# A channel-attention and depthwise-convolution kernel: transposes and head products laid between convolution products, attention's channels turned by 96

## The chip, the cores and the metric

The kernel runs on one core of one Trainium2 chip. Times are device microseconds (us) of one execution. The time before is 2817.3 us, the median of three runs (2817.22 to 2821.58). One further execution was taken with the hardware profiler; all lines with the name of an engine in them come from that one.

## What is computed

The input x has 384 channels of 192 x 192 pixels in float32. The program has two layers, each added to its own input:

```
n   = groupnorm(x, 32 groups)
qkv = 1x1 convolution of n, 384 -> 1152 channels
qkv = max over 2x2 pixels              # 96 x 96 pixels remain
qkv = depthwise 3x3 convolution
q, k, v = split(qkv)                   # 384 channels each, 8 heads of 48
attn = (q/|q|) @ (k/|k|)^T * temperature       # 48 x 48 for each head
out  = sum over 4 of  softmax(top-k of attn) @ v * a
x   = x + 1x1 convolution of repeat2x2(gelu(out)), 384 -> 384
x   = x + depthwise 7x7 convolution(groupnorm(x))
```

The attention matrix is between channels, not pixels: for each head a 48 x 48 matrix that is summed over all 9216 pooled pixels. Only after the last pixel can attention be applied to v.

## The kernel before, in words

Channels lie on the 128 partitions, so 384 channels are three tiles, `KT = 3`. The work comes in stages.

The first stage (to about 170 us) reads x for the statistics of the first norm and scales the 1x1 weights `wq` by them.

The **q/k stage** (to 1355 us) goes over 24 blocks of 8 image rows (`NB = 24`), in the loop `for b in range(NB + 1)`, and in each over six channel tiles `ct` (three of q, three of k). `pooled` makes the 1x1 convolution: three groups of 512 pixels, each three matrix products of 128 x 128 by 512 (L639) that add up in one PSUM tile `pq` (four buffers), and then a maximum over 2 x 2 pixels on VectorE (L647) into a ring of rows. A product in float32 appears in the trace as two instructions, a transpose as one. `depthwise` runs one block behind: nine multiply-adds on VectorE (L680, L682) give the tile `qk` of 128 channels by 384 pixels (nine buffers). When all six tiles of a block are there, `products` (L687 to L717) follows: ScalarE squares each of them for the norms (L691); then for each of three groups of 128 pixels TensorE transposes q's three tiles and k's three tiles into PSUM (L700, tile `tr`, three buffers), ScalarE copies each three to SBUF (L706, tiles `qkT0` and `qkT1`, two buffers each), and TensorE multiplies them (L709) into `grams`. The constant `SPAN` says which k channels a tile of 128 q channels meets: heads are 48 wide and don't end at 128, so the three products of a pixel group have 144, 192 and 144 columns. They add up in one PSUM bank over all blocks.

The loop's last turn (`b == NB`) has no q/k block to convolve. Its depthwise tiles and products remain, and six products of the v stage (`convolve`, tile `xv_begun`) are begun there.

`attention` (L769 to L862) turns `grams` into weights: a row of scales for k along the free dimension (`rkb`), scaled grams, ten small DMAs that bring each head's 48 columns to its q rows (`att`), ranks by comparing all pairs, four masked softmaxes mixed into `mix`, ten DMAs that lay them block-diagonally into `diag`, and seven transposes whose results are copied to `attnT`. It is a generator whose steps are written between the v products of the first three row blocks.

The **v stage** (to about 2195 us) goes over 16 row blocks, six groups of two image rows each, in an order that begins at row block 13 (`FIRST`). For each there are nine `convolve` calls (L537, three for each pair of groups) with a maximum on VectorE (L543), the depthwise 3x3 (L905, L909), `attend` (L961): for each half of the pixels and each tile of output channels the products of `attnT` with those tiles of v that hold a head in common, then gelu on ScalarE (L968); `project` (L985), the residual sum (L1022) and writes to HBM. The list `near` says which tiles meet: channel tiles 0, 1 and 2 meet two, three and two tiles of v, seven products for each half, each of 288 columns. Here most of the order is written by hand: `keep` is `tc.keep_in_program_order`, and the loop over `i` lists what follows what on TensorE and VectorE. The last three row blocks of attention lie behind the loop.

The **last stage** makes the second norm and the 7x7 convolution as matrix products (L1428).

Where `keep` isn't used, the tile framework orders the instructions of each engine when it builds the program, from its own estimate of what is ready; each engine then runs its list in order. `tc.issue_after(ins)` puts an engine's instructions behind `ins`.

The core of the products before is this:

```
for mt, (lo, hi) in enumerate(SPAN):
    last = nc.tensor.matmul(
        gram[mt],
        sides[0][:, mt * P : (mt + 1) * P],
        sides[1][:, lo:hi],
        start=False, ...
```

Of the kernel before, what the change touches and what calls it, by code (L numbers as in the profile page):

```python
# [8 lines left out]
F32 = mybir.dt.float32  # L9
AF = mybir.ActivationFunctionType  # L10
ALU = mybir.AluOpType
AX = mybir.AxisListType

P = 128
C = 384
KT = C // P
# [5 lines left out]
HC = C // HEADS  # L22
# [4 lines left out]
NB = PS // PR  # L27
IR = 2 * PR
BLK = IR * HW
PB = PR * PS  # L30
SUB = BLK // 512
NX = 3
GN_EPS = 1e-5


SPAN = []
for _mt in range(KT):
    _lo = (_mt * P) // HC * HC
    _hi = ((_mt + 1) * P - 1) // HC * HC + HC
    SPAN.append((_lo, _hi))  # L40

PIECES = []
for _mt in range(KT):
# [29 lines left out]
UT = 2  # L73
# [5 lines left out]
def conv_preact_d2(  # L79
# [17 lines left out]
    nc = tc.nc  # L97
# [16 lines left out]
    ident = const.tile([P, P], F32, name="ident")  # L114
# [31 lines left out]
    wp = const.tile([P, KT, C], F32, name="wp")  # L146
# [79 lines left out]

    ssq = const.tile([P, 2 * KT, NB], F32, name="ssq")
    attnT = const.tile([P, KT, C], F32, name="attnT")


    bctx = ExitStack()
# [26 lines left out]

    psx = ExitStack()
    pgram = psx.enter_context(tc.tile_pool(name="pgram", bufs=1, space=PSUM))  # L260
    gram = []
    for mt, (lo, hi) in enumerate(SPAN):
        o = sum(h - l for l, h in SPAN[:mt])
        gram.append((o, o + hi - lo))
    grams = pgram.tile([P, gram[-1][1]], F32, name="grams")
    gram = [grams[:, lo:hi] for lo, hi in gram]
    ptr = psx.enter_context(tc.tile_pool(name="ptr", bufs=3, space=PSUM))
    qx = ExitStack()
    pq = qx.enter_context(tc.tile_pool(name="pq", bufs=4, space=PSUM))
# [19 lines left out]
    keep = tc.keep_in_program_order  # L289
    with tc.tile_pool(name="stp", bufs=1) as stp, tc.tile_pool(name="xsp", bufs=5) as xsp:  # L290
# [19 lines left out]
        whole = stp.tile([P, P], F32, name="whole")  # L310
# [175 lines left out]
        w = wq[:, TWO, i * C : (i + 1) * C]  # L486
        nc.scalar.mul(w, w, rstd0[:, TWO : TWO + 1])
    with tc.issue_after(loaded):
        nc.sync.dma_start(wp, wprojT.rearrange("(t p) o -> p t o", p=P))

# [58 lines left out]
    with ExitStack() as bx:  # L551
        padp = bx.enter_context(tc.tile_pool(name="padp", bufs=1))
        qkp = bx.enter_context(tc.tile_pool(name="qkp", bufs=9))
        trp = bx.enter_context(tc.tile_pool(name="trp", bufs=2))

        gwp = bx.enter_context(tc.tile_pool(name="gwp", bufs=1))

# [66 lines left out]
        for ct in range(2 * KT):  # L624
            ring.append(padp.tile([P, 3 * PR + 2, PS + 2], F32, name=f"ring{ct}"))

        def pooled(b, ct, xb):
            rows = xb.rearrange("p t (r c) -> p t r c", c=HW)
            t = ring[ct]
            r0 = 1 + b % 3 * PR  # L630
            for g in range(3):
                begun, there = sums_qk.pop((b, ct, g), (None, False))
                ps = begun
                if not there:
                    ps = pq.tile([P, 512], F32, name=f"pq{b}_{ct}_{g}", tag="pq")
                    if begun is not None:
                        nc.scalar.copy(ps, begun)
                for kt in range(KT) if begun is None else (TWO,):
                    nc.tensor.matmul(  # L639
                        ps,  # L640
                        wq[:, kt, ct * P : (ct + 1) * P],
                        rows[:, kt, :, g * 64 : (g + 1) * 64],
                        start=(kt == 0),
                        stop=(kt == KT - 1),
                        skip_group_check=begun is not None,
                    )
                nc.vector.tensor_reduce(  # L647
                    t[:, r0 : r0 + PR, 1 + g * 32 : 1 + (g + 1) * 32],
                    ps.rearrange("p (h a w b) -> p h w a b", h=PR, a=2, b=2),
                    AX.XY,  # L650
                    ALU.max,
                )
# [32 lines left out]
            r0 = b % 3 * PR  # L685
            taps(dst, ct, lambda i, j: ring[ct][:, r0 + i : r0 + i + PR, j : j + PS])

        def products(b, qk):
            for i in range(2 * KT):
                junk = trp.tile([P, PB], F32, name=f"junk{b}_{i}", tag="junk")  # L690
                nc.scalar.activation(  # L691
                    junk, qk[i].rearrange("p h w -> p (h w)"), AF.Square,
                    accum_out=ssq[:, i, b : b + 1],
                )
            for j in range(PB // P):
                sides = []
                for s in range(2):
                    ps = ptr.tile([P, C], F32, name=f"tr{b}_{j}_{s}", tag="tr")
                    for i in range(KT):
                        nc.tensor.transpose(  # L700
                            ps[:, i * P : (i + 1) * P],
                            qk[s * KT + i].rearrange("p h w -> p (h w)")[:, j * P : (j + 1) * P],
                            ident,
                        )
                    sb = trp.tile([P, C], F32, name=f"qkT{b}_{j}_{s}", tag=f"qkT{s}")
                    nc.scalar.copy(sb, ps)  # L706
                    sides.append(sb)
                for mt, (lo, hi) in enumerate(SPAN):
                    last = nc.tensor.matmul(  # L709
                        gram[mt],  # L710
                        sides[0][:, mt * P : (mt + 1) * P],
                        sides[1][:, lo:hi],
                        start=False,
                        stop=(b == NB - 1 and j == PB // P - 1),
                        skip_group_check=True,
                    ).ins
            return last  # L717


        nc.tensor.matmul(  # L720
            grams, z[:, RUN : RUN + P], z[:, RUN : RUN + grams.shape[1]], start=True, stop=False,
            skip_group_check=True,
        )
        for b in range(NB + 1):
            xb = None
            if b < NB:
                xb = held.pop(b) if b in held else load_x(b, "xq")
            else:

                qx.close()  # L730
                pv = psx.enter_context(tc.tile_pool(name="pv", bufs=2, space=PSUM))
                xb = xpool.tile([P, 2 * UT, KT, RB * HW], F32, name="xv_begun", tag="xb")
                for kt in range(KT):
                    nc.sync.dma_start(xb[:, :, kt], image_rows(kt, order[0], 0, 2 * UT))
            qk = []
            for ct in range(2 * KT + 1):
                if b < NB and ct < 2 * KT:
                    if b == 0 and ct < 2:

                        if ct == 0:  # L740
                            pooled(b, 0, xb)
                            pooled(b, 1, xb)
                            biases()
                    else:
                        pooled(b, ct, xb)
                    bordered(b, ct)
                if b > 0 and ct > 0:
                    dst = qkp.tile([P, PR, PS], F32, name=f"qk{b}_{ct}", tag="qk")
                    qk.append(dst)
                    depthwise(b - 1, ct - 1, dst)  # L750
                    if ct == 2 * KT:
                        multiplied = products(b - 1, qk)
                    if b == NB:
                        with tc.issue_after(multiplied):
                            for n in ((), (), (0, 1), (), (2, 3), (4,), (5,))[ct]:
                                t0 = n // KT * UT
                                convolve(0, t0, n % KT, xb[:, t0 : t0 + UT], lambda ins: ins)
            if b == 2:
                for tiles in vrows:
                    row_borders(tiles)  # L760
            if b < len(pieces):
                with tc.issue_after(stats0):
                    weights(*pieces[b])

    xctx.close()

    near = {}

    def attention(ap):  # L769

# [13 lines left out]
        along_free(rkb, rn[:, KT : 2 * KT], ptr, "rk", "tr")  # L784
        yield

        scaled = ap.tile([P, KT, C // 2], F32, name="scaled")
        for mt, (lo, hi) in enumerate(SPAN):
            nc.vector.scalar_tensor_tensor(
                scaled[:, mt, 0 : hi - lo], gram[mt], rn[:, mt : mt + 1], rkb[:, lo:hi],  # L790
                ALU.mult, ALU.mult,
            )
        att = ap.tile([P, KT, HC], F32, name="att")
        for i, (mt, r0, r1, h) in enumerate(PIECES):
            eng = (nc.gpsimd, nc.scalar)[i % 2]
            o = h * HC - SPAN[mt][0]
            eng.dma_start(att[r0:r1, mt, :], scaled[r0:r1, mt, o : o + HC])
        yield


# [50 lines left out]
            eng.dma_start(diag[r0:r1, mt, h * HC : (h + 1) * HC], mix[r0:r1, mt, :])  # L851
        yield
        for dt in range(KT):
            cts = [ct for ct in range(KT) if SPAN[ct][0] < (dt + 1) * P and SPAN[ct][1] > dt * P]
            near[dt] = cts
            ps = ptr.tile([P, C], F32, name=f"aT{dt}", tag="tr")
            for ct in cts:
                nc.tensor.transpose(
                    ps[:, ct * P : (ct + 1) * P], diag[:, ct, dt * P : (dt + 1) * P], ident
                )  # L860
            lo, hi = cts[0] * P, (cts[-1] + 1) * P
            nc.vector.tensor_copy(attnT[:, dt, lo:hi], ps[:, lo:hi])  # L862

# [85 lines left out]
    def attend(i, pin=lambda ins: ins):  # L951
# [2 lines left out]
        gl = gp.tile([P, KT, PBC], F32, name=f"gl{b}", tag="gl")  # L954
        for h in range(2):
            for ct in range(KT):
                dts = [dt for dt in range(KT) if ct in near[dt]]
                ps = ptr.tile([P, C], F32, name=f"po{b}_{ct}_{h}", tag="tr")
                for dt in dts:
                    keep(  # L960
# [563 lines left out]
```

## Time and profile before

| what | before |
|---|---|
| median of three runs | 2817.3 us |
| the profiled execution | 2802.07 us |
| its span, first to last instruction | 2800.4 us |
| TensorE clock granted, mean | 0.994 |
| q/k transposes (L700) | 432 instructions, 273 ns each in the middle |
| gram products (L709) | 432 instructions: 288 of 144 columns, 144 of 192 |
| copies of transposes (L706) | 144 on ScalarE, 478 ns each |
| attention times v (L961) | 448 instructions of 288 columns |
| projection (L985) | 576 instructions of 288 columns |

A row of groups gives line, engine, operation, the tile written and those read, shapes and count, then busy time and the mean duration of one in ns, then idle time of the engine ahead of it and what ended it. On TensorE the instructions are pipelined: the duration of one is longer than the distance from its start to the next one's start, and that distance is what it costs in a full stream. A row of the timeline gives start, length, engine, line and count; neighbours of one kind are merged. PEld is TensorE's loading of the stationary operand, which can run beside a product.

### The profile page before, as it was taken

Reading aid. Unit: us, or ns where it says so; the run is one execution under the profiler, and the core shown is the slowest. Engines: PE = TensorE matmul, PEld = TensorE weight load, DVE = VectorE, ACT = ScalarE, POOL = GpSimd, SP = SyncE. Lnnn points to the kernel's source line nnn. Section 1 sums busy time; section 2 is a strip of 40 time slices with the busy share of each in tenths; the row PEclk is TensorE's granted clock in tenths of the full one; section 3 lists DMA queues with packets and bytes.
Section 4 is the critical chain, followed back from the end, with each engine's and each line's share of the span. In section 5 each row is a group of like instructions: output and inputs, shape, how many; then the busy total and the mean of one; then the engine's idle time right before and its main releaser. Section 6 shows DMA issues by size and latency. Waiting matters only on the chain. (4 is left out here: it accounts for less than half of the span.)

```text
span 2800.4 us, 25638 instructions
## 1 busy us (share of the span) xinstructions
PE 2646.0 (94%) x8717; PEld 1588.6 (57%) x8717; DVE 2324.8 (83%) x3383; ACT 873.3 (31%) x1638; POOL 748.0 (27%) x884
## 2 busy tenths in 40 slices
PE   0399999999999999999999999999999899999998
PEld 0144444445445444444556666666666677777776
DVE  7989887887878878878798988889889678887786
ACT  0141111111111111111202232222323577777776
POOL 1023443100000000000102231010101477877777
PEclk9999999999999999999999999999999999999999
DMA  9976666401001001010235998575664899999998
GB/s 381 400 248 216 227 203 219 165 34 68 34 34 68 34 35 67 34 62 7 78 127 174 334 379 314 171 249 196 209 236 152 321 341 360 374 367 370 367 376 265
DMA packets 234002, 580.98 MB, mean 207 GB/s; under 512 B 16608, under 2 KB 165712, under 8 KB 217104
## 3 DMA queue, kind: packets, MB, share of 16 engines
q1 hardware_dynamic: 173376, 283.44, 28.8%
q0 software_dynamic: 37376, 148.85, 15.2%
q10 hardware_dynamic: 23120, 147.07, 14.0%
q8 instruction: 69, 1.13, 0.2%
q14 instruction: 61, 0.50, 0.0%
HBM read 370.93 MB, written 208.21 MB: 207 GB/s over the span
## 5 line engine op out<-in xcount | busy, mean ns | idle before, releaser
L639 PE MATMUL pq<-xq,wq 128*128 128x512 f32 x2268 | 990.7, 593 | 0.0
L639 PEld LDWEIGHTS pq<-xq,wq 128*128 128x128 f32 x2268 | 423.9, 190 | 491.3 <-issue 446.5
L682 DVE SCALAR_TENSOR_TENSOR qk<-ring,wd,qk 128x384 f32<-128x384 f32 x1152 | 674.8, 613 | 20.9 <-ACT ring L669 7.1
L537 PE MATMUL pv<-xv,wq 128*128 128x384 f32 x1656 | 539.8, 487 | 2.5 <-DVE rows L543 1.4
L647 DVE TENSOR_REDUCE ring<-pq 128x128 f32<-128x512 f32 x428 | 293.9, 688 | 193.5 <-PE pq L639 192.0
L1428 PE MATMUL pc<-main,w 128*128 128x288 f32 x1536 | 436.2, 407 | 3.9 <-POOL aux L1348 1.7
L537 PEld LDWEIGHTS pv<-xv,wq 128*128 128x128 f32 x1656 | 314.8, 190 | 218.6 <-DVE rows L543 3.0
L1448 DVE TENSOR_SCALAR apart<-pc,rb 32x576 f32<-32x576 f32 x384 | 312.2, 813 | 108.9 <-PE pc L1428 97.1
L1428 PEld LDWEIGHTS pc<-main,w 128*128 128x128 f32 x1536 | 290.8, 190 | 87.3 <-issue 2.1
L1446 ACT ACTIVATE apart<-pc,rb 32x576 f32<-32x576 f32 x384 | 281.1, 732 | 137.2 <-PE pc L1428 132.4
L905 DVE SCALAR_TENSOR_TENSOR vb<-rows,wd,vb 128x576 f32<-128x576 f32 x384 | 313.2, 817 | 11.2
L1428 PE MATMUL pc<-aux,h 128*128 128x288 f32 x768 | 249.5, 407 | 3.1 <-issue 2.4
L691 ACT ACTIVATE junk<-qk 128x384 f32<-128x384 f32 x144 | 75.3, 523 | 544.0 <-DVE qk L682 544.0
L1387 POOL COPY res<-apart 128x1152 f32<-128x1152 f32 (+1 forms) x96 | 218.4, 2305 | 48.6 <-DMA out_dram<-res 40.2
L773 POOL TENSOR_TENSOR rn<-rn,halfpos 128x6 f32<-128x6 f32 x1 | 1.4, 1360 | 850.6 <-DVE rn L772 850.6
L1022 DVE TENSOR_TENSOR sx<-xr,y 128x576 f32<-128x576 f32 x180 | 203.7, 1173 | 26.9 <-ACT y L993 21.2
L1063 POOL DMA_DIRECT2D sd<-sx x96 | 72.2, 755 | 491.8 <-DVE sx L1022 472.6
L543 DVE TENSOR_REDUCE rows<-pv 128x192 f32<-128x768 f32 x144 | 137.8, 957 | 55.7 <-PE pv L537 55.6
L1428 PEld LDWEIGHTS pc<-aux,h 128*128 128x128 f32 x768 | 145.6, 190 | 45.2 <-issue 4.4
L1042 ACT ACTIVATE wq<-sx,negmid 128x1152 f32<-128x1152 f32 x96 | 120.6, 1256 | 95.4 <-DVE sx L1022 91.2
L1271 DVE SCALAR_TENSOR_TENSOR w<-eye,sb,w 128x512 f32<-128x512 f32 x96 | 144.1, 1540 | 1.5
L985 PE MATMUL pr<-gl,wp 128*128 128x288 f32 x576 | 142.6, 407 | 0.0
(226 smaller groups left out, 2113.6 us busy)
## 6 DMA issues: line engine op xcount, KB each, us to landing
sd<-sx POOLq DMA_DIRECT2D x96, 600.0 KB, 9.9
out_dram<-res SPq DMA_DIRECT2D x192, 288.0 KB, 10.7
main<-sd ACTq DMA_DIRECT2D x46, 1200.0 KB, 5.1
xv<-in_x_dram SPq DMA_DIRECT2D x138, 384.0 KB, 6.5
xr<-in_x_dram SPq DMA_DIRECT2D x45, 1152.0 KB, 12.0
xq<-in_x_dram SPq DMA_DIRECT2D x21, 2304.0 KB, 8.2
w<-wt ACTq DMA_DIRECT2D x46, 1024.0 KB, 6.9
xs<-in_x_dram SPq DMA_DIRECT2D x24, 1536.0 KB, 15.6
```

What stands on the lines that cost most here:

```text
L537: nc.tensor.matmul(ps[:, u, 0 : RB * HW], wq[:, kt, o : o + P], xb[:, u, kt, :], start=(kt == 0), stop=(kt == KT - 1),)
L639: nc.tensor.matmul(ps, wq[:, kt, ct * P : (ct + 1) * P], rows[:, kt, :, g * 64 : (g + 1) * 64], start=(kt == 0), stop=(kt == KT - 1), skip ...
L647: nc.vector.tensor_reduce(t[:, r0 : r0 + PR, 1 + g * 32 : 1 + (g + 1) * 32], ps.rearrange("p (h a w b) -> p h w a b", h=PR, a=2, b=2), AX. ...
L682: nc.vector.scalar_tensor_tensor(dst, src, w, dst, ALU.mult, ALU.add)
L905: pin(nc.vector.scalar_tensor_tensor(dst, src, w, dst, ALU.mult, ALU.add))
L985: nc.tensor.matmul(ps[:, 0:H], wp[:, ct, ot * P : (ot + 1) * P], gl[:, ct, h * H : (h + 1) * H], start=(ct == 0), stop=(ct == KT - 1),)
L1022: nc.vector.tensor_tensor(bass.AP(flat.tensor, flat.offset + at(e) + a * RUN, [flat.ap[0], [JP, NT], [1, NJ], [at(f) - at(e), 2]],), xq[:, ...
L1271: nc.vector.scalar_tensor_tensor(mid, eye.unsqueeze(1).to_broadcast([P, 4, P]), sb[:, c : c + 1], mid, ALU.mult, ALU.add,)
L1387: keep(copy(res[ps, k], apart[ps, :, k].rearrange("p e n -> p n e")))
L1428: nc.tensor.matmul(ahead[q][:, k, 0 : NT * NJ], lhs, rhs, start=(j == 0), stop=(j == 2), skip_group_check=True,)
L1446: keep(nc.scalar.mul(dst, src, scale))
L1448: keep(nc.vector.tensor_scalar_mul(dst, src, scale))
```

## The change

For q and k, products are now taken of two heads at a time: `PAIR` is 96 channels, and 96 q channels meet exactly the same 96 k channels, so a pixel group has four products of 96 x 96 for the three before. The result lies in partitions 0 to 95 of `grams`, four pairs side by side in 384 columns.

`products` is split. `squares` follows each depthwise tile. `turned` (the transposes and copies) and `products` become generators, put into a list `between`; `pinned` keeps the q/k convolution products in program order and takes one step of the list behind each of them: one transpose, or one product. The three q tiles of a block are transposed behind the first channel tile of the block after next's convolution, the k tiles behind the fourth, the twelve products behind those. The transposed sides hold a whole block (three pixel groups) in one buffer each. In the last turn the block before the last one's steps lie between the begun v products, and the last block's come after them in one go.

For v, the output channels of attention are turned by 96 (`TURN`): tile 0 holds channels 96 to 223, tile 1 224 to 351, tile 2 352 to 383 and 0 to 95. Each then meets two tiles of v (`MEET`), six products for each half. `attnT` is cleared once and written only where heads lie, and the rows of the projection's weights are loaded in the turned order by three DMAs. In `attention` the scaling by k's norms is one operation on 96 partitions, and the scaling by q's norms comes after the ten DMAs.

```diff
+PAIR = 2 * HC
+TURN = PAIR
+MEET = [...]
...
+    nc.gpsimd.memset(attnT, 0.0)
...
-    gram = [grams[:, lo:hi] for lo, hi in gram]
+    grams = pgram.tile([P, C], F32, name="grams")
...
-        nc.sync.dma_start(wp, wprojT.rearrange("(t p) o -> p t o", p=P))
+        whole = (C - TURN) // P
+        nc.sync.dma_start(
+            wp[:, 0:whole], wprojT[TURN : TURN + whole * P].rearrange("(t p) o -> p t o", p=P)
+        )
+        over = C - TURN - whole * P
+        nc.sync.dma_start(wp[0:over, whole], wprojT[C - over :])
+        nc.sync.dma_start(wp[over:P, whole], wprojT[0:TURN])
...
-        trp = bx.enter_context(tc.tile_pool(name="trp", bufs=2))
+        trp = bx.enter_context(tc.tile_pool(name="trp", bufs=1))
...
+        between = []
+        def pinned(ins):
+            if ins.ins.engine != mybir.EngineType.PE:
+                return ins
+            keep(ins)
+            while between and next(between[0], between) is between:
+                between.pop(0)
+            return ins
...
+                    if b > 1:
+                        pinned(ins)
...
+        def squares(b, ct, t):
+            junk = trp.tile([P, PB], F32, name=f"junk{b}_{ct}", tag="junk")
+            nc.scalar.activation(junk, t, AF.Square, accum_out=ssq[:, ct, b : b + 1])
+        def turned(b, s, side, qk):
+            for j in range(PB // P):
+                ps = ptr.tile([P, C], F32, name=f"tr{b}_{j}_{s}", tag="tr")
+                for i in range(KT):
+                    keep(
                         nc.tensor.transpose(
+                            ps[:, i * P : (i + 1) * P], qk[i][:, j * P : (j + 1) * P], ident
                         )
+                    )
+                    if i == KT - 1:
+                        nc.scalar.copy(side[:, j], ps)
+                    yield
+        def products(b, sides):
+            nonlocal multiplied
+            for j in range(PB // P):
+                for lo in range(0, C, PAIR):
+                    multiplied = keep(
+                        nc.tensor.matmul(
+                            grams[0:PAIR, lo : lo + PAIR],
+                            sides[0][:, j, lo : lo + PAIR],
+                            sides[1][:, j, lo : lo + PAIR],
+                            start=False,
...
+                    ).ins
+                    yield
...
+            done, qk = qk, []
             for ct in range(2 * KT + 1):
+                for s, at in enumerate((0, KT) if b < NB else (0, KT + 1)):
+                    if ct == at and done:
+                        if s == 0:
+                            sides = []
+                        sides.append(
+                            trp.tile([P, PB // P, C], F32, name=f"qkT{b}_{s}", tag=f"qkT{s}")
+                        )
+                        between.append(turned(b - 2, s, sides[s], done[s * KT : (s + 1) * KT]))
+                        if s == 1:
+                            between.append(products(b - 2, sides))
...
-                        with tc.issue_after(multiplied):
-                            for n in ((), (), (0, 1), (), (2, 3), (4,), (5,))[ct]:
-                                t0 = n // KT * UT
-                                convolve(0, t0, n % KT, xb[:, t0 : t0 + UT], lambda ins: ins)
+                        for n in ((), (), (0, 1), (), (2, 3), (4,), (5,))[ct]:
+                            t0 = n // KT * UT
+                            convolve(0, t0, n % KT, xb[:, t0 : t0 + UT], pinned)
+                        if ct == 2 * KT:
...
+                            for s in range(2):
+                                between.append(turned(b - 1, s, sides[s], qk[s * KT :]))
+                            between.append(products(b - 1, sides))
+                            for left in between:
+                                for _ in left:
+                                    pass
...
-            nc.vector.scalar_tensor_tensor(
-                scaled[:, mt, 0 : hi - lo], gram[mt], rn[:, mt : mt + 1], rkb[:, lo:hi],
-                ALU.mult, ALU.mult,
-            )
+        nc.vector.tensor_tensor(scaled[0:PAIR], grams[0:PAIR], rkb[0:PAIR], ALU.mult)
...
-            eng.dma_start(att[r0:r1, mt, :], scaled[r0:r1, mt, o : o + HC])
+            o = mt * P - h // 2 * PAIR
+            eng.dma_start(att[r0:r1, mt, :], scaled[o + r0 : o + r1, h * HC : (h + 1) * HC])
+        nc.vector.tensor_tensor(
+            att, att, rn[:, 0:KT].unsqueeze(2).to_broadcast([P, KT, HC]), ALU.mult
+        )
...
-            nc.vector.tensor_copy(attnT[:, dt, lo:hi], ps[:, lo:hi])
+            for l, h in ((lo, min(hi, TURN)), (max(lo, TURN), hi)):
+                if l < h:
+                    o = (l - TURN) % C
+                    nc.vector.tensor_copy(attnT[:, dt, o : o + h - l], ps[:, l:h])
...
-                dts = [dt for dt in range(KT) if ct in near[dt]]
+                dts = MEET[ct]
```

## Prediction

> **What bounds the kernel now.** First the page's engine shares and slices. From the third slice on TensorE (PE) is full at full clock, in the q/k stage (to 1355 us) and in the v stage (to 2133 us); VectorE (DVE) is below it.
>
> ```profile
> PE 2646.0 (94%) x8717; PEld 1588.6 (57%) x8717; DVE 2324.8 (83%) x3383; ACT 873.3 (31%) x1638; POOL 748.0 (27%) x884
> PE   0399999999999999999999999999999899999998
> PEclk9999999999999999999999999999999999999999
> ```
>
> Then the waits of q/k (window 200 to 1355): DVE waits for PE, PE for nearly nothing.
>
> ```profile
> DVE ring L647 <- PE pq L639: 187.8, 129, 1.9
> DVE qk L682 <- ACT ring L669: 7.1, 21, 0.3
> ```
>
> So time is PE's count of columns, and I read prices as differences of neighbouring starts. The timeline of PE around two block ends (start, length, count):
>
> ```profile
> 741.92 1.50 PE L700 MATMUL tr<-ident,qk 128*128 128x128 f32 x10
> 743.25 1.02 PE L639 MATMUL pq<-xq,wq 128*128 128x512 f32 x2
> 744.12 0.49 PE L700 MATMUL tr<-ident,qk 128*128 128x128 f32 x3
> ...
> 792.96 1.50 PE L700 MATMUL tr<-ident,qk 128*128 128x128 f32 x10
> ...
> 795.48 1.02 PE L639 MATMUL pq<-xq,wq 128*128 128x512 f32 x2
> 796.53 0.44 PE L700 MATMUL tr<-ident,qk 128*128 128x128 f32 x2
> ...
> 797.67 1.84 PE L709 MATMUL grams<-qkT,qkT 128*128 128x144 f32 x12
> 799.34 0.49 PE L700 MATMUL tr<-ident,qk 128*128 128x128 f32 x3
> 799.67 0.60 PE L639 MATMUL pq<-xq,wq 128*128 128x512 f32 x1
> ```
>
> Two convolution instructions take 0.86 us (743.25 to 744.12), so 0.429 each; a product in f32 is two instructions. Three transposes take 0.33 us, so 0.109 each, one instruction. The twelve gram instructions take 1.67 us: eight of 144 columns at 0.122 and four of 192 at 0.162 (their rows' means, 291 and 327 ns, differ by the same 0.04) are 1.62, the rest is a wait. A block lasts 51.04 us (741.92 to 792.96); first and last block end lie at 230.19 and 1355.53, so the mean is 1125.34 / 22 = 51.15.
>
> In v the same view gives 0.243 us for an instruction of 288 columns and 0.323 for 384; one row block lasts 50.35 us, all PE:
>
> ```profile
> 1589.27 6.96 PE L961 MATMUL po<-vb,attnT 128*128 128x288 f32 x28
> 1596.06 11.78 PE L537 MATMUL pv<-xv,wq 128*128 128x384 f32 x36
> 1607.67 8.89 PE L985 MATMUL pr<-gl,wp 128*128 128x288 f32 x36
> 1616.40 23.38 PE L537 MATMUL pv<-xv,wq 128*128 128x384 f32 x72
> 1639.62 0.65 PE L961 MATMUL po<-vb,attnT 128*128 128x288 f32 x2
> ```
>
> The windows of v (engine sums, then clock, DMA share, GB/s) show the one other full resource, in two row blocks:
>
> ```profile
> 1588.00:1639.00 51.00, 51.00 (x176) 33.13 (x175) 45.60 (x53) 13.76 (x30) 18.62 (x25) 1.00 1.04 383
> 1742.00:1792.00 50.00, 50.00 (x173) 32.53 (x172) 44.79 (x51) 13.77 (x30) 4.50 (x6) 1.00 0.63 211
> ```
>
> **What the Trainium skill says.** "TensorE: Matmul & The Clock Gate", section LDWEIGHTS: loading takes the weight's columns over 1.2 GHz whatever its rows, so 0.107 us for 128 and 0.080 for 96. The trace agrees for 128: thirty one-column bias products (176.71 to 179.98 us) take 0.109 each, so the load sets the pace. No load of 96 columns is in this trace. Same page, Part 2, step 1: the next load is pulled ahead under the running matmul. The trace agrees: after a transpose a convolution starts 0.109 us later, its load hidden. Same page, Part 1, "Architectural detail", engine queue depths: ScalarE (ACT) is strict FIFO; this matters for a rival. "Perfetto Trace Analysis", Roofline: 16 DMA engines give a core some 435 GB/s at most; the 383 above with a share of 1.04 is near it.
>
> **q and k, the work itself.** A block now is 108 convolution instructions x 0.429 = 46.33, 18 transposes x 0.109 = 1.96, and 3 x 2 x (0.122 + 0.162 + 0.122) = 2.44 of grams: 50.73. The mean is 51.15, so 0.42 are waits at the block's end for copies and last taps (as from 795.48 to 796.53 above: 1.05 us for two convolution instructions, 0.86).
> Added: 12 products of 96 columns for 9. The rows fit 0.833 ns per column plus 0.002 to 0.003, so one instruction streams in 0.083. Laid singly between convolutions, the first of the pair is followed by its own second half's load of 96 columns (0.083), the second by a convolution's load of 128, which 0.083 doesn't hide: 0.112. So 0.195 a product, 12 x 0.195 = 2.34: only 0.10 less than now. Bounds: if a 96-column load costs as much as 128, 0.224 each, 2.69; if loads hide wholly, 0.166, 1.99.
> Transposes are as many; 0.109 holds beside convolutions already. Waits: operands are a block old and the copies spread over the block, but the first product stands one convolution (0.86 us) behind the last k transpose, whose copy takes 0.48 on ACT plus pipeline. I keep half of today's, 0.21; bounds 0.05 and 0.60. New block: 46.33 + 1.96 + 2.34 + 0.21 = 50.84, 0.31 less. 22 blocks have their products laid in: **7 us** (bounds: 22 x (51.15 - 51.58) = -9 and 22 x (51.15 - 50.33) = +18).
> Squares are now written behind their own channel tile: same count on ACT, which already takes them as DVE finishes each tile. DVE's 41 of 51 us are unchanged. The q/k tiles' nine buffers suffice, since the q tiles are read in the first of six channel tiles.
>
> **The turn from q/k to v.** From the last q/k convolution's end (1355.5) to the end of the six v products begun there (1393.0) are 37.5 us. After: 72 x 0.323 = 23.3; 36 transposes 3.9; 12 products laid in 2.3; 12 in a row at 2 x 0.083, 2.0; the small temperature and norm products that lie there now 1.5; 1.0 for the last maxima, as v takes over their PSUM before any transposes cover it; 0.9 for copies at the drain, whose six at 0.43 outlast the transposes. Sum 34.9: **2.6 us** (0 to 5). If cover fails there, DVE's last q/k taps (1375) are late next; they end before the drain. The attention chain now starts with those products done, some 4 us later against PE's v products; today its matrix is ready at 1478.5 and first used at 1488.6, so that slack covers it.
>
> **v.** Six products for seven per half: 2 x 2 x 0.243 = 0.97 us per row block, 13 row blocks in the loop: 12.6. DVE has 44.8 of then 49.4 us and is next late, not yet. Two row blocks run at a DMA share of 1.04 (a 2 us wait for an input tile at 1668 follows); there a shorter PE only waits, so I take off 1.9: **10.7** (bounds 8 and 12.6). The last three row blocks (2133 to 2193) wait for DVE and ACT: 0.3 of 2.9.
>
> **Small things at nothing.** Clearing attnT on POOL is 1.07 us (the row of the equal diag memset) before the first statistics, while PE waits 97 us for input; without that cover 1.1. Projection weights in three DMAs for one: SP's queue at 166 us, the next q/k load is gated by blocks ending at 230; uncovered about 1 us. Attention's scaling: one operation for three (0.97), plus a multiply of 128x144 (0.3, as L829 of that shape), five small copies for three, within the chain's slack.
>
> **Sum.** 7 + 2.6 + 10.7 + 0.3 = 20.6. The profiled execution took 2802.07 us (span 2800.4, 1.7 around it), so 2781.5; the three runs' median lies 15.2 above it, which I take as unchanged: 2817.3 - 20.6 = **2796.7**.
>
> **Rivals.**
> - A, all covers hold, loads hide, waits vanish: 18 + 5 + 12.6 + 2.9 = 38, 2779. For it: PE's spacings are regular to a few nanoseconds. Against: the 0.109 floor of the bias products.
> - B, q/k gives nothing: loads at 0.112 and waits of 0.42 make 22 x (51.15 - 51.40) = -6; with 2 and 10: 2811. For: no 96-column load was seen.
> - C, slower: the ACT queue. A copy of the last k transposes falls behind a square, which waits for its taps; PE, now in a fixed order, stands at the first product and all convolutions queue behind it. For: ACT idles 544 us ahead of squares waiting for DVE, and a copy (L706) did run right behind a square (L691) that it had no need of:
>
> ```profile
> 744.87 0.52 ACT L691 ACTIVATE junk<-qk 128x384 f32<-128x384 f32 x1 [1.37 <-DVE qk L682]
> ...
> 745.61 0.86 ACT L706 COPY qkT<-tr 128x384 f32<-128x384 f32 x2
> ```
>
> Against: waits at block ends, this among them, cost PE 0.42 us in all. From 20.6 / 22, 0.94 us per block beyond my 0.21, it eats the whole gain; half a tile's taps (2.7 us) gives 59 - 21 = 38 slower, 2855.
> - D, v gives nothing, as DVE's order or DMA sets the row block: 2817.3 - 9.9 = 2807. Against: DVE's waits in v are for PE.
>
> **How the numbers follow.** Forecast 0.62, A 0.10, B 0.12, C 0.08, D 0.08. Two parts in a thousand (5.6 us) is about what can be told from no change. B's and D's tails fall within that; a third of B and an eighth of D are put there, the rest of them at faster: faster 0.62 + 0.10 + 0.08 + 0.07 = 0.87, same 0.05, slower 0.08. The range 2782 to 2811 takes in the forecast with the inner part of its bounds, D and half of B, and leaves out A's end and C.
>
> **What would show it.** Block period 50.6 to 51.0; gram instructions starting 0.083 and 0.112 apart; waits of PE for copies under 0.3 per block; row blocks of 49.4, the two at full DMA still 50.3 or with waits; turn near 35. Gram spacings of 0.112 both mean B; a recurring wait of PE for qkT over 1 us means C.

## The result and the profile after

The changed kernel took 2806.5 us (median of seven runs, 2803.1 to 2807.6) beside 2817.3 for the kernel before: a ratio of 0.9954, 95% interval 0.9938 to 0.9971, so 11 us were gained by the medians (8 to 17 by the interval) where 20.6 were forecast. Later both ran once more, on another chip: the kernel before took 2798.4 and the changed one 2785.7, 0.9953 again (0.9940 to 0.9965), a gain of 12.7 us. The experiments below ran on that chip and on a third; neither kernel ran again on the first. Ratios below are against the kernel before in the same session.

TensorE is still full; the gap in its 24th slice is new. From the page of the changed kernel:

```profile
PE 2630.5 (94%) x8797; PEld 1555.7 (55%) x8797; DVE 2328.5 (83%) x3383; ACT 874.2 (31%) x1638; POOL 752.8 (27%) x885
PE   0399999999999999999999979999999899999998
```

In q/k (waits of VectorE, window 200 to 1348) VectorE waits for TensorE as before, and for the transposes' reading of its old tiles, L725, which is new and costs TensorE nothing:

```profile
DVE ring L673 <- PE pq L663: 185.6, 106, 2.2
DVE qk L706 <- PE tr L725: 18.0, 43, 0.8
DVE qk L708 <- ACT ring L695: 4.7, 14, 0.3
```

TensorE's timeline in a block (start, length, count) shows what lies between:

```profile
772.69 0.27 PE L725 MATMUL tr<-ident,qk 128*128 128x128 f32 x1
772.80 1.02 PE L663 MATMUL pq<-xq,wq 128*128 128x512 f32 x2
773.66 0.33 PE L739 MATMUL grams<-qkT,qkT 128*96 128x96 f32 x2
773.83 1.05 PE L663 MATMUL pq<-xq,wq 128*128 128x512 f32 x2
774.72 0.33 PE L739 MATMUL grams<-qkT,qkT 128*96 128x96 f32 x2
```

A transpose costs 0.11 (772.69 to 772.80). A pair product takes 0.17 to the next convolution, but that one then takes 0.89 (773.83 to 774.72) and not 0.86: start by start, 0.083 and 0.085 for the product's two instructions, and 0.458 for 0.429 between the convolution's two. The sum, 0.083 + 0.085 + 0.029, is 0.197. The period is 50.72 in every block (51.15 before), and TensorE's waits for copies in q/k are gone.

In v the row block is as forecast, until 1650. Starts of TensorE, 1583.70 to 1633.08 being 49.38:

```profile
1583.70 5.98 PE L1014 MATMUL po<-vb,attnT 128*128 128x288 f32 x24
1589.52 11.77 PE L549 MATMUL pv<-xv,wq 128*128 128x384 f32 x36
1601.13 8.89 PE L1038 MATMUL pr<-gl,wp 128*128 128x288 f32 x36
1609.86 23.38 PE L549 MATMUL pv<-xv,wq 128*128 128x384 f32 x72
1633.08 5.98 PE L1014 MATMUL po<-vb,attnT 128*128 128x288 f32 x24
...
1650.51 8.89 PE L1038 MATMUL pr<-gl,wp 128*128 128x288 f32 x36
1676.47 1.62 PE L549 MATMUL pv<-xv,wq 128*128 128x384 f32 x2 [17.06 <-DMA xv<-in_x_dram]
1681.08 1.65 PE L549 MATMUL pv<-xv,wq 128*128 128x384 f32 x2 [3.00 <-DMA xv<-in_x_dram]
1685.55 24.71 PE L549 MATMUL pv<-xv,wq 128*128 128x384 f32 x68 [2.82 <-DMA xv<-in_x_dram]
```

Three waits for an input tile, 22.9 us, where the profile of before had 1.1 (27.6 and 1.9 when the late starts around them are counted). The late starts are products at a lower granted clock (the rate that TensorE was given): the two at 1676.47 take 1.62 us, and such a pair took 0.81 at 1350.85. The clock is the column ahead of the DMA share in this line:

```profile
1660.00:1692.00 32.00, 9.71 (x16) 4.60 (x17) 5.53 (x6) 3.96 (x10) 5.88 (x8) 0.57 1.04 370
```

The window 1560 to 1700 of the first profile of before, then of after:

```profile
1560.00:1700.00 140.00, 138.85 (x475) 89.88 (x474) 123.02 (x138) 40.70 (x88) 46.83 (x63) 1.00 1.00 362
```

```profile
1560.00:1700.00 140.00, 117.12 (x380) 73.38 (x379) 102.33 (x115) 35.24 (x74) 43.47 (x59) 0.90 0.99 341
```

DMA is full in both, but moved 6% less in the second. It moved less ahead of the first wait already: from 1584 to 1633 it was 364 GB/s, where the same kernel in the same window later moved 388 on the other chip (shares 1.03 and 1.04).

### The profile page after: what moved, and what is told of

The parts are those of the page before. It is cut to its first block, busy times and chain, and to the rows that moved or that the text cites. A ratio compares the mean times of both kernels' runs of the same rounds, so it can differ in the third digit from the quotient of the medians.

```text
span 2805.9 us, 25852 instructions
## 1 busy us (share of the span) xinstructions
PE 2630.5 (94%) x8797; PEld 1555.7 (55%) x8797; DVE 2328.5 (83%) x3383; ACT 874.2 (31%) x1638; POOL 752.8 (27%) x885
## 5 line engine op out<-in xcount | busy, mean ns | idle before, releaser
L663 PE MATMUL pq<-xq,wq 128*128 128x512 f32 x2268 | 1064.1, 596 | 0.0
L708 DVE SCALAR_TENSOR_TENSOR qk<-ring,wd,qk 128x384 f32<-128x384 f32 x1152 | 656.2, 615 | 11.3 <-ACT ring L695 4.7
L663 PEld LDWEIGHTS pq<-xq,wq 128*128 128x128 f32 x2268 | 382.2, 191 | 350.0 <-issue 321.7
L549 PE MATMUL pv<-xv,wq 128*128 128x384 f32 x1656 | 545.5, 490 | 28.0 <-DMA xv<-in_x_dram 22.9
L1440 POOL COPY res<-apart 128x1152 f32<-128x1152 f32 (+1 forms) x96 | 221.2, 2330 | 12.4 <-ACT apart L1499 8.5
L555 DVE TENSOR_REDUCE rows<-pv 128x192 f32<-128x768 f32 x144 | 137.7, 957 | 75.9 <-PE pv L549 75.8
L739 PEld LDWEIGHTS grams<-qkT,qkT 128*96 128x96 f32 x576 | 92.1, 163 | 136.9 <-issue 135.2
L1324 DVE SCALAR_TENSOR_TENSOR w<-eye,sb,w 128x512 f32<-128x512 f32 x96 | 161.0, 1715 | 1.5
```

Of the source, the lines that this page charges most:

```text
L549: nc.tensor.matmul(ps[:, u, 0 : RB * HW], wq[:, kt, o : o + P], xb[:, u, kt, :], start=(kt == 0), stop=(kt == KT - 1),)
L555: nc.vector.tensor_reduce(rows[ct][:, 1 + t0 : 1 + t0 + UT, 1 : PS + 1], ps[:, :, 0 : RB * HW].rearrange("p u (a w b) -> p u w a b", a=2, ...
L663: ins = nc.tensor.matmul(ps, wq[:, kt, ct * P : (ct + 1) * P], rows[:, kt, :, g * 64 : (g + 1) * 64], start=(kt == 0), stop=(kt == KT - 1) ...
L708: nc.vector.scalar_tensor_tensor(dst, src, w, dst, ALU.mult, ALU.add)
L1324: nc.vector.scalar_tensor_tensor(mid, eye.unsqueeze(1).to_broadcast([P, 4, P]), sb[:, c : c + 1], mid, ALU.mult, ALU.add,)
L1440: keep(copy(res[ps, k], apart[ps, :, k].rearrange("p e n -> p n e")))
```

## The experiments

**Both kernels once more, and both without the halo writes.** Theory T: the TensorE work taken away is real, and the crowded row blocks give most of it back. Rival R: these waits aren't the reason.

The kernel before, and the changed kernel, with no edit:

> The kernel before, unchanged, profiled once more. Theory T (the 22 us of TensorE work taken away are real, and waits for input tiles in the two v row blocks at full DMA, 2 us in the first profile of before and 25 us in that of after, give most of them back; these waits differ from run to run): the time is again near 2817, and this profile, if its own time is near 2817 as well, shows 10 to 20 us of waits of the v products for xv between 1590 and 1700. Rival R (the waits belong to the change; the kernel before is simply slower in unprofiled runs): waits for xv stay near 2 us and the profile stays near 2802.

> The changed kernel, profiled once more. T: q/k block period 50.65, row blocks of 49.38 outside the crowded stretch, and waits for xv between 10 and 30 us, another number than the 25 of the first profile; time 2803 to 2808. R: the waits are 25 us again.

Measured: 2796.7 (ratio 0.9996, 0.9988 to 1.0004; the profile's own time 2796.7) and 2785.7. Waits for xv, counted by starts: 1.1 and 2.8 us. So the changed kernel doesn't bring 28 us of waits with it everywhere: R's "25 again" fell. T's guess on before fell too, as it now ran at 2797 with hardly a wait. On the first chip the waits were probably in every run of the changed kernel: all seven show a mean granted clock of 0.987 or 0.988, as the profiled one (0.987), and on the other chip its five show 0.991 to 0.993. The stretch at 0.57 above lowers the mean by 0.005 (an estimate: 0.43 x 32 of 2806 us), which is the difference. Whether it was the chip, no run tells. In the same window the changed kernel moved 378 GB/s, with little waiting:

```profile
1560.00:1700.00 140.00, 137.99 (x463) 87.42 (x462) 124.93 (x143) 37.38 (x80) 45.44 (x61) 1.00 1.03 378
```

These two profiles are what I compare by stage below. The first is its kernel's median, the second the slowest of five, 1.5 us over the median.

```diff
-            if r >= TR - HALO:
-                halos.append(((r - TR + HALO) * NQ, -JP))
-            if r < HALO:
-                halos.append((BOT - TOP + r * NQ, JP))
```

and zeros written to the same rows of `sh` in the q/k stage by 18 DMAs:

> The kernel before without the writes of halo rows in the residual step (27.6 MB in four row blocks, to sh); zeros are written there in the q/k stage, where DMA is at a share of 0.12, so the image's inner borders are left out of the second layer. T: the waits for xv vanish, so unprofiled time falls by 12 to 20 us, to 2797 to 2805. R: falls by 0 to 3 us.

> The changed kernel with the same writes left out. T: falls by some 25 us, to 2776 to 2784, so the change is worth 19 to 24 us where DMA isn't full: q/k 8, v 12.6, the rest the turn between. R: the change is worth 11 us here too, 2790 or more.

Measured: 2813.0 and 2796.2. Both rose: the zeros went out at once and delayed one q/k input by some 17 us (16.3 in before's variant, 17.4 in after's, from the waits of TensorE). The crowd had been moved, not taken away, so these times alone tell nothing of T and R. TensorE's wait in the changed kernel's variant:

```profile
PE pq L669 <- DMA xq<-in_x_dram: 17.4, 1, 17.4
```

Yet in v the edit did its work: no wait for xv in either. With it the difference of the two kernels is 16.8 us, against 12.7 for the unedited pair in the same session (T said 19 to 24, R 11), and the row blocks (first attention product to last v product) differ by 642.6 - 630.2 = 12.4, the 12.6 of the removed products. In the unedited pair it is 643.7 - 633.0 = 10.7. T holds for the mechanism, not for its size: on this chip the crowd cost 1.7 us of the gain, in the first profiles some 26.

**The turn of v undone.** `TURN = 0`, and the projection's weights loaded in one piece in plain order:

> The changed kernel with the turn of attention's channels undone (TURN = 0: seven products for each half again); q and k as changed. T: row blocks of 50.35 for 49.38, so 11 to 13 us more than the changed kernel, waits for xv about as in before on the same chip; q/k stage as changed. R (v's products aren't what sets the row block, DMA or VectorE does): row blocks stay near 49.4 to 49.6 and the time within 3 us of the changed kernel.

Measured: 2793.0, ratio 0.9982 (0.9974 to 0.9989), so 7 to 8 us over the changed kernel. Its row blocks take 645.4, 12.4 more, with the same waits (2.8), and one is 50.35 again (1789.92 to 1840.27). The other 4 us are in the last stage, 664.0 for 668.3, which scatters by as much (below). R fell.

```profile
1817.05 23.38 PE L543 MATMUL pv<-xv,wq 128*128 128x384 f32 x72
1840.27 6.95 PE L1008 MATMUL po<-vb,attnT 128*128 128x288 f32 x28
1847.06 8.23 PE L543 MATMUL pv<-xv,wq 128*128 128x384 f32 x25
```

**Pairs, not laid between.** `go` runs all steps that are left, at the end of a block. (In the text on record, "week-old" should read "block-old".)

```diff
-            keep(ins)
-            while between and next(between[0], between) is between:
-                between.pop(0)
-            return ins
+            return keep(ins)
...
+            go()
```

> The changed kernel with pairs and week-old operands kept (a block's products are still taken a block late), but not laid between: transposes and products of a block follow in one go behind the next block's convolution. T (lateness, not laying, takes the waits away): block period 46.33 + 4.47 (what the last block's steps took in one go) = 50.8, 0.15 over the laid one, 3 us in 22 blocks. R (laying between products is what hides the copies): 51.1 to 51.3, 10 us or more over the changed kernel.

Measured: the block period is 50.81 in the mean, as T has it, 0.09 over the laid one; each chunk takes 0.3 to 0.5 us more than its instructions at their pace. The whole took 2799.6 (1.0000, 0.9988 to 1.0013), 14 over the changed kernel, where T had 3, and little of that is in the blocks: in the turn to v the chunks stand in a row, TensorE loses 24 us there (9 in the changed kernel), and the first attention product comes 12 us later. (Its profile, 2791, is the fastest of twelve runs from 2791 to 2807, so where the median's other 9 us lie isn't seen.) So laying between is worth 2 us in the blocks; taking operands a block late had already removed most waits. It is worth more at the turn, in the order that the framework then chose.

**Wide products, laid between.**

```diff
-                for lo in range(0, C, PAIR):
+                for mt, (lo, hi) in enumerate(SPAN):
...
-                            grams[0:PAIR, lo : lo + PAIR],
-                            sides[0][:, j, lo : lo + PAIR],
-                            sides[1][:, j, lo : lo + PAIR],
+                            gram[mt],
+                            sides[0][:, j, mt * P : (mt + 1) * P],
+                            sides[1][:, j, lo:hi],
```

> The changed kernel with the three wide products (144, 192 and 144 columns) in place of the four of 96, still laid between. T (a product of 96 columns costs 0.197 laid, as its second half is too short to hide the next load of 128 columns; a wide one hides it): block period 46.33 + 1.96 + 9 laid products of 2.44 = 50.74, so 0.09 more than with pairs, 2 us in all. R (pairs are the gain in q/k): 51.0 or more, 8 us.

Measured: period 50.81 for 50.72, T's 0.09. Behind a wide product the convolution's two instructions lie 0.429 apart, not 0.458. So in q/k the pairs are worth 2 us. The whole was faster, 2778.0 (0.9930, 0.9913 to 0.9947): its turn to v is 4 us shorter, of which below, and its last stage 7 us (661.5), which is scatter.

**Four products laid together.** One `yield` for each pixel group instead of one for each product:

> The changed kernel with a pixel group's four products laid behind one convolution product instead of one behind each. T (each laid product delays the convolution's second half by 0.029 us, because its own second half of 0.083 is too short for a load of 128 columns; the convolution's pair then spaces 0.458 for 0.429): only three such delays per block for twelve, block period 46.33 + 1.96 + 3 x (7 x 0.083 + 0.085 + 0.029) = 50.38 for 50.65, 6 us less in 22 blocks. R (the 0.029 comes with every product of 96 columns, laid or not): period 50.65, time unchanged.

Measured: 2776.8, ratio 0.9931 (0.9916 to 0.9946), the fastest of all. The period is 50.48, 0.24 less (0.27 expected with 0.083; inside the row each instruction takes 0.085). Starts:

```profile
769.06 0.84 PE L739 MATMUL grams<-qkT,qkT 128*96 128x96 f32 x8
769.74 1.05 PE L663 MATMUL pq<-xq,wq 128*128 128x512 f32 x2
770.63 0.84 PE L739 MATMUL grams<-qkT,qkT 128*96 128x96 f32 x8
```

Eight instructions in 0.68, then one late convolution (0.89). 5 us of the 9 gained are this; the rest lies ahead of the blocks (2) and in the last stage (3), where the code is the same, and I count it as scatter.

**A wider load for the same product.**

```diff
-                            grams[0:PAIR, lo : lo + PAIR],
-                            sides[0][:, j, lo : lo + PAIR],
+                            grams[0 : min(P, C - lo), lo : lo + PAIR],
+                            sides[0][:, j, lo : min(lo + P, C)],
```

> The changed kernel with 128 columns for 96 in the stationary operand of three of each four pair products (32 rows of output more, which nothing reads). T (the load's column count sets the pace of a short product): first to second half 0.109 to 0.112 for 0.083 in those, so 9 x 0.027 = 0.24 more per block, 5 us in all. R (the load is hidden whatever its columns, the 96 moving columns set the pace): 0.083 again, time unchanged.

Measured: period 50.96, 0.24 more, just T's sum, but not where T put it. First to second half is 0.083 as before; the second half's distance to the convolution grew from 0.085 to 0.1115:

```profile
771.50 0.36 PE L739 MATMUL grams<-qkT,qkT 128*128 128x96 f32 x2
771.70 1.05 PE L663 MATMUL pq<-xq,wq 128*128 128x512 f32 x2
772.58 0.36 PE L739 MATMUL grams<-qkT,qkT 128*128 128x96 f32 x2
```

The loads' columns do set the pace, one load behind the other: 0.085 for the second half's 96 columns, then 0.112 for the convolution's 128, whose last 0.029 shows as the late second convolution instruction. 0.085 + 0.112 is the 0.197. The time, 2787.9, lies 3 us over the changed kernel by the ratios (0.9964 and 0.9953), where 22 blocks make 5; other stages scatter by that.

**Holding the residual's loads back.**

```diff
+    early_v = loads[-1]
...
+        with tc.issue_after(early_v):
             nc.sync.dma_start(xr, image_rows(ot, order[i % NBC], 0, NT))
```

> The changed kernel with the residual's first loads (xr) held on SP's queue until the last of the first three row blocks' v loads is issued. T (in the changed kernel three xr loads of 1152 KB are issued at 1378, ahead of attention's ten small DMAs, which then land 8 us after issue; VectorE's ranks and with them the v maxima wait, TensorE stands 5 us at 1395): the ten land in 3 to 4 us, the wait at 1395 falls to 1 to 2 us and the time by 3 to 5 us. R (the wait is VectorE's own order, the ranks ahead of the maxima): the wait stays 4 to 5 us, time unchanged.

Measured: attention's DMAs land in 1.7 us after issue for 5.0, yet TensorE's wait for the v maxima there is 3.2 us for 3.9. My theory fell, R held for the wait. The wait in the profile of before, then in the changed kernel:

```profile
1402.25 17.99 PE L537 MATMUL pv<-xv,wq 128*128 128x384 f32 x54 [1.36 <-DVE rows L543]
```

```profile
1399.39 4.86 PE L549 MATMUL pv<-xv,wq 128*128 128x384 f32 x9 [3.87 <-DVE rows L555]
```

VectorE's list around it, in the variant:

```profile
1383.31 0.96 DVE L555 TENSOR_REDUCE rows<-pv 128x192 f32<-128x768 f32 x1 [2.67 <-PE pv L549]
1384.31 2.02 DVE L964 TENSOR_SCALAR vb<-rows,wd,bdb 128x576 f32<-128x576 f32 x1
1386.37 1.67 DVE L960 SCALAR_TENSOR_TENSOR vb<-rows,wd,vb 128x576 f32<-128x576 f32 x2
1387.96 0.30 DVE L846 TENSOR_TENSOR att<-att,rn 128x144 f32<-128x144 f32 x1
1388.29 2.56 DVE L865 TENSOR_TENSOR gt<-att 128x2304 f32<-128x2304 f32 x1
1390.77 2.55 DVE L867 TENSOR_TENSOR eq<-att 128x2304 f32<-128x2304 f32 x1
1393.24 0.95 DVE L555 TENSOR_REDUCE rows<-pv 128x192 f32<-128x768 f32 x1
```

Between two maxima (L555) stand three depthwise steps, the new scaling and two comparisons. TensorE has two PSUM buffers, 7.8 us of products, to bridge from one maximum's start to the next one's end. From start to start lie 9.9 us here, 10.6 in the changed kernel, 8.3 in the wide-product variant and 8.1 in the kernel before, the last two without depthwise steps. With 1.0 for the maximum, less 7.8, this gives waits of 3.1, 3.8, 1.5 and 1.3; measured are 3.2, 3.9, 1.6 and 1.4. So the spacing of the maxima sets the wait; that the depthwise steps are what widened it is read from these lists, and no run moved them alone. The wide-product variant's turn is 132.0 for 136.0.

The 3.9 us wait cost more than itself: from 1400 to 1404 the granted clock is 0.57 in both profiles of the changed kernel and 1.00 in both of before, which is some 1.7 us more (0.43 x 4).

The variant with held loads took 2779.2 (0.9933, 0.9916 to 0.9949), mostly by an earlier start of the blocks (4.5 us) and a shorter last stage (3.8): a depthwise step ahead of the blocks (the first line, changed kernel; the second, variant) ran beside GpSimd's clearing of a tile (187.28 to 189.46 in the changed kernel, from 187.79 in the variant) or not:

```profile
187.34 2.33 DVE L706 TENSOR_SCALAR qk<-ring,wd,bdb 128x384 f32<-128x384 f32 x1
```

```profile
186.24 0.48 DVE L706 TENSOR_SCALAR qk<-ring,wd,bdb 128x384 f32<-128x384 f32 x1
```

**Halo rows copied later.** The writes of halo rows in `residual` are replaced, in the loop over `i` from 7 on, by copies within HBM:

```diff
+        nc.gpsimd.dma_start(
+            sh[f],
+            bass.AP(sd.tensor, sd.offset + row * C * RUN + shift, [[RUN, C], [1, RUN]]),
+        )
```

> The changed kernel with the halo rows (27.6 MB in the four crowded row blocks) written later: from row block 7 on they are copied from sd to sh within HBM, some 7 copies of 460 KB per row block. T (the waits for xv in the crowded row blocks are DMA bandwidth): those waits, 3 us on the second chip and 28 on the first, fall under 1; row blocks stay at 49.38 and DMA's share under 0.9; time 2 to 4 us under the changed kernel on a chip like the second, 20 or more on one like the first. R (the waits are SP's order, a load issued behind another that waits): they stay.

Measured: 2790.0 (0.9974, 0.9963 to 0.9985), 6 over the changed kernel by the ratios; waits for xv by starts 7.8 for 2.8. It tells nothing of T and R: without a fixed order the framework put all 60 copies where their input was ready, 1531 to 1705, and DMA stayed full, a row block longer than before. Its windows:

```profile
1584.00:1633.00 49.00, 46.95 (x152) 29.45 (x152) 40.92 (x47) 12.95 (x28) 14.43 (x27) 0.97 1.01 356
1633.00:1683.00 50.00, 50.00 (x171) 32.30 (x170) 45.57 (x53) 13.78 (x30) 9.89 (x18) 1.00 0.99 339
1683.00:1733.00 50.00, 47.05 (x160) 29.83 (x159) 41.84 (x48) 13.78 (x30) 9.99 (x17) 1.00 1.01 347
```

**The three edits together** (four laid together, later copies, held loads):

> The changed kernel with four products laid together, the halo rows copied later and the residual's first loads held back. T: sum of the parts, 6 + 3 + 3 = 12 us under the changed kernel, 2770 to 2776 on a chip where before takes 2798. R (the parts meet the same wait elsewhere): within 5 us of the changed kernel.

Measured: 2781.0, 0.9942 (0.9930 to 0.9955): the sum did not come, and R's 5 us held (4.7). Period 50.48 as with four alone, row blocks 638.6 for 633.0, as with the copies alone (638.0).

## Why the prediction was right in kind and short in size

By stage, from the second pair of profiles (spans 2795.0 and 2785.5), each number a difference of first or last starts:

| stage | before | changed | difference | forecast |
|---|---|---|---|---|
| to the end of the second block's convolution | 230.2 | 232.8 | +2.6 | 0 |
| q/k, 22 blocks | 1124.7 | 1115.4 | -9.3 | -7 |
| turn, to the first attention product | 133.5 | 136.0 | +2.6 | -2.6 |
| row blocks, to the last v product | 643.7 | 633.0 | -10.7 | -10.7 |
| the rest | 662.9 | 668.3 | +5.4 | -0.3 |

- **q/k, right.** A laid product was put at 0.195 and measured 0.197; the bound at which a short product hides the load wholly (0.166) is out. The load of 128 columns was put at 0.112 with no line behind it, as the bias products had given 0.109; the wider load later gave 0.1115. The starts of 0.083 and 0.112 named as a sign didn't come: they are 0.083 and 0.085, and the rest shows one instruction later. Waits were put at 0.21 a block and are nothing (4.6 us in 22 blocks), and the block's own work is 0.09 over the sum (50.72 for 50.63): 2 us more gained than forecast. Half of the 0.09 stands behind the 18 transposes, where the convolution's second instruction is late too (0.432 for 0.429), so the load that I read as hidden there was not wholly so. Rivals B and C are out: ScalarE's squares never stood ahead of a copy long enough to stop TensorE.
- **v, right on the later chip.** 0.97 per row block, less a loss of 1.7 to DMA in the crowded ones (1.9 forecast). On the first chip that loss is the mis-sized term: "there a shorter PE only waits, so I take off 1.9" was priced from one profile, and the profile of after shows 28 us of waits. Why DMA moved 341 GB/s there, and 362 to 378 in the others, no run shows. Two rivals were not tested: that the first chip differs, and that an input's load stands behind another one in SyncE's queue. The first profile of before, 15 us under its median, was no measure of it either; whether its timed runs held such waits is open. So the first 11 us can't be split by stage, and that they lie near the later 12.7 may be chance.
- **The turn, wrong.** The failed step is "the attention chain now starts with those products done ... that slack covers it". The first part came: from the last convolution to the end of the temperature and norm products it takes 35.2 (34.9 forecast). But then VectorE's list had the chain's comparisons, and with them three depthwise steps, ahead of one of v's maxima; TensorE stood 4 us at 1395 for 1.4 before, and some 1.7 us more went to the lower clock after. This part is 4.9 us longer than in the kernel before. I had asked if the chain would be late for its user, not whom its steps stand in front of. Held loads did not mend it.
- **The rest.** +2.6 at the start and +5.4 at the end come from code that the change hardly touches, and I had given no term to either. Over the ten later profiles of the changed kernel and its variants, whose code in these stages is nearly the same, the first lies between 228.1 and 232.8 and the last between 660.7 and 668.3. The two are of different kinds. The end scatters between executions: the two profiles of before have 667.3 and 663.0, the two of the changed kernel 663.3 and 668.3, so +5.4 says nothing of the change. The start repeats within 0.1 us in both profiles of each kernel, so it belongs to the order that the framework built. There the step beside GpSimd took 2.33 us for 1.87 before, TensorE waited 2.0 for 1.7, and from 190 to 200 the granted clock was 0.83 in both profiles of the changed kernel and 1.00 in both of before, some 1.7 us. Together they are about as large as the parts of the forecast.
- Rival A (2779) is out by q/k's load floor; rival D by the row blocks of 49.38. The kernel with four products laid together came within 2 us of the forecast's 20.6 (22 us by its medians), in part by another way than the one forecast and in part by the scatter above.

## What to carry to other kernels

Where one engine is full, count its columns and loads: 0.97 us per row block came just as counted. A short product laid between long ones pays for the next full load, so lay several behind one, and operands a block old take more waits away than the laying does. Where a transfer or another engine is nearly full beside it, price it over several executions, and ask of each step that comes earlier whom it now stands in front of.

## What the runs showed of the hardware

Two f32 instructions of 96 columns between long ones cost 0.197 us, one load behind the other: 0.085 for a load of 96 columns and 0.112 for one of 128. The "TensorE: Matmul & The Clock Gate" page of the Trainium skill, section LDWEIGHTS, prices a load by its columns (0.080 us for 96, 0.107 for 128); these runs agree within 5 ns. What I had not expected is where it shows: the convolution begins on time, and its second instruction is late (0.458 for 0.429).

Behind TensorE's waits of 3.2 to 3.9 us in the turn the granted clock fell (0.57 over 4 us in the changed kernel); behind those of 1.4 us in the kernel before it did not. At the start it fell behind a wait of 2.0 us and not behind one of 1.7.
